# A planner's durations: other lengths for stores and loads, for products side by side, and for VectorE beside GpSimd

## The chip, the cores and the metric

The kernel runs on one core of one Trainium2 chip. The metric is the device time of one execution in microseconds (us). A core has TensorE (PE: matmuls and transposes; its weight loads are shown as PEld), VectorE (DVE), ScalarE (ACT), GpSimd (POOL) and SyncE (SP, which issues most DMAs). Each engine has a queue of instructions of its own, which it works off in order. Engines wait for one another by semaphores only.

## The reference, cut to what matters

Four layers run one after the other on x, 4 batches of 512 tokens by 512 channels in fp32, each conditioned on a vector of 512 per batch.

```
L0  h = LN(x)*(1+scale)+shift
    q = rope(h Wq^T) (16 heads of 32); c = h Wkd^T; k, v = c Wku^T, c Wvu^T (4 kv heads)
    x = x + softmax(window/global/causal-block mask of q k^T) v Wo^T
L1  RMS norm; 8 query heads of 64, one kv head, rope;  x += attention Wo^T
    RMS norm; x += (silu(h Wg^T) * (h Wu^T)) Wd^T          (width 2048)
L2  LN with scale and shift; q, k, v = h Wqkv^T + bias (16 heads of 32)
    q, k normalized to length 1 a head, q times exp(min(mul, log 100))
    x += gate1 * (softmax(q k^T + bias) v Wproj^T + b)
    x += gate2 * (gelu(h Wfc1^T + b) Wfc2^T + b)            (width 2048)
L3  8 groups of 64 channels, each: y = gelu(x W1 + b1) W2 + b2   (64 -> 256 -> 64)
    x = x + silu(LN(y)*(1+scale)+shift) out_W + out_b
```

The result is x, (4, 512, 512) in fp32.

## The kernel before, in words

All operands are fp32. A *product* is a 128x512 result built from four matmuls of 128x128 weights and 512 columns each; the trace shows each such matmul as two records. A softmax's probabilities are turned by 128x128 transposes on TensorE (`tr`, L360) into a PSUM bank, copied to SBUF as pT (`evict`, ACT or VectorE), and used as weights. Scores have 32 or 64 rows only, and four (or two) such products stand side by side in the array; so do the products of pT and v, which have 32 or 64 columns.

**Two streams.** The work of each batch is cut into stages: a01 (L0 and L1's attention), m1 (L1's MLP), a2 (L2's attention), m2 (L2's MLP and L3), for the last batches in halves. Stream A takes attention, stream M the MLPs of another batch, so that products of one fill TensorE while the softmax of the other runs. A stage is a Python generator that yields between steps; `interleave()` picks the next step. Weights come by 1 MB loads into two rings (tiles wa and wm). PSUM holds two pairs of banks for scores (tile two) and two single banks for each stream (tile bank). x has a ring of three buffers, in which stream M also keeps its kT and v.

**The planner.** Nothing is sent to an engine at once. `Clocks` (L161) writes down every operation with a planned start. `written` and `vacant` say from when an operand is there and from when a buffer is free, by the marks of earlier operations; `length` gives an operation's planned duration; `gap` looks for the first gap in the engine's list that is long enough; `plan` puts these together; `run` records an operation of ACT, VectorE, GpSimd or a DMA (all of these appear as L301 in the profile, loads as L367); `matmul` does the same for TensorE, with one running time `now` (matmuls appear as L354). `evict` plans a copy on ACT and on VectorE and takes the one that ends earlier. A stage's step is ready when its `Until` time is reached, so planned times also choose which step comes next. At the end all operations are sorted by planned start and emitted in that order (`tc.manual_schedule()`). The planned times are thus not waited for on the chip: they fix only the order of each engine's queue, the choice of ACT or VectorE, and, through the order, which buffer is reused when. What an engine really waits for are the data and buffers of the instruction at the head of its queue.

**Places that the prediction's steps touch.**

- a2's attention (`attention2`, with `attention` and `turn_full`): four scores products of 32 rows into two PSUM pairs (`two<-kT,nq`); on VectorE a custom instruction that adds the bias and takes the row's maximum (`probs<-two,late`, twice per half of the scores, and its accumulator's read neg); exponentials on ACT; the reciprocal inv; probs times inv on GpSimd; 16 transposes in four banks, each copied to pT. Products of stream M stand between.
- L2's normalization: q or k (tile t or mt), its squares, the sum ss on VectorE, a power on GpSimd (inv), t times inv on VectorE, transposes of t.
- `norm_steps`: statistics st and mv of x on VectorE, a power on GpSimd (rstd), then four tensor_scalar (nq or mn) with x from SBUF.
- L0's attention at the start (`attention0`): scores `two<-x,mn` (mn and x hold q and k there), maxima and exponentials into wm, wm times inv on GpSimd, transposes into hid. Products `bank<-wa_q,h` of batch 1's side go between, and they need the transposed nq (h).
- The load of a batch's x (`x<-in_x`) into a buffer of the ring, and the stores `out<-x`.

Of the kernel before, what the change touches and what calls it, by code (L numbers as in the profile page):

```python
# [58 lines left out]
class Ring:  # L59
# [3 lines left out]
    def __init__(self, load, made, pool, dram, tag, n, names):  # L63
        self.made, self.held = made, {}
        self.fetch, self.pool, self.dram, self.tag, self.n = load, pool, dram, tag, n
        self.names, self.tiles, self.taken, self.ahead = names, [], 0, n
# [94 lines left out]
class Clocks:  # L161
# [6 lines left out]

    def __init__(self):
        self.now, self.tiling, self.tables, self.queue = 0.0, None, None, 0.0  # L170
        self.busy = {"DVE": [], "ACT": [], "POOL": []}
        self.fixed, self.rings, self.program = {}, {}, []

# [38 lines left out]
    def gap(self, engine, ready, length):  # L212

        t = ready
        for a, b in self.busy[engine]:
            if b > t:
                if a - t >= length:
                    break
                t = b
        return t  # L220

    def length(self, engine, op, outs, ins, func):

        n = max(math.prod(v.shape[1:]) for v in outs[:1] + ins[:1])
        if engine == "DVE":
            held = 0.08 + (0.00073 if op == "tensor_scalar" and len(ins) > 1 else 0.00104) * n
        elif engine == "ACT":
            held = 0.03 + 0.00088 * n + (0.24 if len(outs) > 1 else 0.0)
            if func in self.SET and self.SET[func] != self.tables:
                held += self.LOAD_TABLE  # L230
        elif func == "pow":
            held = 0.3 + 0.157 * n
        else:
            held = 0.06 + (0.0023 if op == "tensor_tensor" else 0.0012) * n
        return held, held + 0.09

    def plan(self, engine, op, outs, ins, func=None):
        ready = max([self.written(*ins)] + [self.vacant(o) for o in outs])
        held, length = self.length(engine, op, outs, ins, func)
        return self.gap(engine, ready, held), held, length  # L240

    def run(self, engine, op, outs, ins, emit, func=None):
        if op == "dma_start":
            start = max([self.now, self.queue, self.written(*ins)] + [self.vacant(o) for o in outs])
            self.queue = start + max(math.prod(v.shape) for v in outs + ins) * 4 / 3.0e5
            end = self.queue + 2.0
        else:
            start, held, length = self.plan(engine, op, outs, ins, func)
            if func in self.SET:
                self.tables = self.SET[func]  # L250
            spans = [s for s in self.busy[engine] if s[1] > self.now - 60.0] + [(start, start + held)]
            self.busy[engine], end = sorted(spans), start + length
        for x in ins:
            self.mark(x, end + self.HOP, False)
        for x in outs:
            self.mark(x, end + self.HOP, True)
        self.program.append((start, len(self.program), emit))

    def matmul(self, out, left, right, begins, emit, turn=False):

        tiling = tuple(32 if n <= 32 else 64 if n <= 64 else 128 for n in (left.shape[0], math.prod(left.shape[1:])))
        if turn:
            tiling = (128, 128)
        start = max(self.now, self.written(left) + self.WEIGHTS, self.written(right))
        if out.tile.fresh and out.tile.before:
            start = max(start, out.tile.before.last)
        n = math.prod(right.shape[1:])
        self.now = start + (0.00085 if turn else 0.001676) * n * tiling[0] * tiling[1] / 16384
        if tiling != self.tiling:
            self.now += 0.2  # L270
        self.tiling = tiling
        self.mark(left, self.now, False)
        self.mark(right, self.now, False)
        self.mark(out, self.now + self.TAIL + self.HOP, True)
        self.program.append((start, len(self.program), emit))


# [31 lines left out]
def cond_seq_kernel(ctx: ExitStack, tc: tile.TileContext, a: dict, out: bass.AP):  # L309
# [66 lines left out]
    def evict(dst, src):  # L376

        ends = [(start + length) for start, _, length in (clocks.plan(e, "copy", [dst], [src]) for e in ("ACT", "DVE"))]
        if ends[0] <= ends[1]:
            scalar.copy(dst, src)  # L380
        else:
            vector.tensor_copy(dst, src)
# [1347 lines left out]
```

## Time and profile before

| what | value |
| --- | --- |
| three runs | 2469.41, 2475.03, 2479.4 us; median 2475.03 |
| the profiled execution, its own time | 2479.07 us |
| its span, from the first to the last instruction | 2477.3 us |
| mean granted TensorE clock | 0.991 |
| busy: ACT, GpSimd | 865.2 us (35%), 726.5 us (29%) |
| DMA | 154.17 MB, 62 GB/s on average |
| a 1 MB weight load, issue to landing | 5.1 to 5.7 us |

The profile shows each engine's busy time, the chain of instructions that ended last, and for each instruction how long its engine had been idle before it and what ended that. In rows of the timeline the columns are: start in us, duration in us (of all instructions that the row puts together), engine, line, operation, output<-input without buffer numbers, shapes, how many instructions, and in brackets the idle time before with its releaser. The durations of matmul records overlap: a record of 512 columns shows about 0.6 us, while the next one starts 0.43 us after it. A row with x8 is eight records. L301, L354, L360 and L367 are the lines of helpers that emit all recorded operations, so the tiles' names tell which step it is.

### The profile page before, as it was taken

Reading aid. Unit: us, or ns where it says so; the run is one execution under the profiler, and the core shown is the slowest. Engines: PE = TensorE matmul, PEld = TensorE weight load, DVE = VectorE, ACT = ScalarE, POOL = GpSimd, SP = SyncE. Lnnn points to the kernel's source line nnn. Section 1 sums busy time; section 2 is a strip of 40 time slices with the busy share of each in tenths; the row PEclk is TensorE's granted clock in tenths of the full one; section 3 lists DMA queues with packets and bytes.
Section 4 is the critical chain, followed back from the end, with each engine's and each line's share of the span. In section 5 each row is a group of like instructions: output and inputs, shape, how many; then the busy total and the mean of one; then the engine's idle time right before and its main releaser. Section 6 shows DMA issues by size and latency. Waiting matters only on the chain.

```text
span 2477.3 us, 33249 instructions
## 1 busy us (share of the span) xinstructions
PE 2413.0 (97%) x12564; PEld 1254.1 (51%) x12564; DVE 1123.4 (45%) x2902; ACT 865.2 (35%) x2076; POOL 726.5 (29%) x920
## 2 busy tenths in 40 slices
PE   7999999999999999999899999999999999999998
PEld 4555654444554555544355455554455544554444
DVE  5656552133653444534354444454455333653233
ACT  2745441003550442413354053332255203551312
POOL 5633320004322223323232221433232203532221
PEclk9999999999999999999899999999999999999999
DMA  3221212220113112120221212111211221112210
GB/s 110 69 73 52 85 35 85 85 72 35 39 48 106 52 52 70 40 74 27 76 68 39 86 52 75 49 56 56 85 35 52 83 92 51 35 54 84 72 56 22
DMA packets 83311, 154.17 MB, mean 62 GB/s; under 512 B 3584, under 2 KB 10784, under 8 KB 83152
## 3 DMA queue, kind: packets, MB, share of 16 engines
q1 hardware_dynamic: 82544, 151.83, 18.0%
q8 instruction: 100, 1.64, 0.3%
q14 instruction: 59, 0.48, 0.1%
q0 software_dynamic: 176, 0.15, 0.0%
q10 hardware_dynamic: 432, 0.07, 0.0%
HBM read 147.83 MB, written 4.21 MB: 61 GB/s over the span
## 4 chain that ended last, share of the span: by engine, by line
PE 91%; DVE 4%; ACT 2%; issue 1%; DMA 1%; POOL 1%; SPq 0%; POOLq 0%; DVEq 0%; ACTq 0%
PE bank L354 70%; PE bank L360 11%; PE two L354 10%; DVE probs L301 1%; ACT probs L301 1%; DVE pT L301 1%; PE two L360 0%; DVE nq L301 0%; ACT wm L301 0%; DVE mx L301 0%; DMA out<-x 0%; DMA wm<-in_units 0%; DMA x<-in_x 0%; POOL probs L301 0%; DVE mt L301 0%
## 5 line engine op out<-in xcount | busy, mean ns | idle before, releaser
L301 POOL TENSOR_SCALAR probs<-probs,inv 128x512 f32<-128x512 f32 (+4 forms) x544 | 316.4, 596 | 676.7 <-DVE inv L301 632.3
L301 ACT ACTIVATE probs<-probs,neg 128x512 f32<-128x512 f32 (+2 forms) x448 | 265.5, 594 | 221.0 <-DVE neg L301 212.4
L360 PEld LDWEIGHTS bank<-ident,probs 128*128 128x128 f32 (+2 forms) x1744 | 203.7, 141 | 175.0 <-issue 138.0
L360 PE MATMUL bank<-ident,probs 128*128 128x128 f32 (+2 forms) x1744 | 246.9, 276 | 8.0 <-DVE pT L301 7.0
L354 PE MATMUL bank<-mT,wm_gate 128*128 128x512 f32 x512 | 247.9, 596 | 0.0
L354 PE MATMUL bank<-mT,wm_up 128*128 128x512 f32 x512 | 247.6, 601 | 0.0
L354 PE MATMUL bank<-wm_down,hid 128*128 128x512 f32 x496 | 232.5, 597 | 0.0
L301 DVE CUSTOM_DVE_ANT_0 probs<-two,late 128x512 f32<-128x512 f32 x256 | 166.4, 688 | 80.1 <-PE two L354 47.1
L354 PE MATMUL bank<-wm_fc,hid 128*128 128x512 f32 x384 | 189.5, 593 | 0.0
L354 PE MATMUL bank<-mT,wm_fc 128*128 128x512 f32 x384 | 182.9, 595 | 0.0
L301 ACT COPY pT<-bank 128x512 f32<-128x512 f32 (+2 forms) x259 | 145.7, 577 | 78.2 <-PE bank L360 69.9
L354 PE MATMUL two<-kT,nq 32*128 32x512 f32 (+5 forms) x1088 | 150.5, 537 | 1.3 <-ACT probs L301 0.8
L301 ACT ACTIVATE mt<-bank 128x512 f32<-128x512 f32 x64 | 37.9, 591 | 318.5 <-PE bank L354 318.5
L301 DVE TENSOR_TENSOR x<-x,bank 128x512 f32<-128x512 f32 x98 | 66.8, 682 | 173.9 <-PE bank L354 173.9
L354 PEld LDWEIGHTS bank<-mT,wm_up 128*128 128x128 f32 x512 | 91.4, 191 | 100.1 <-issue 99.6
L354 PEld LDWEIGHTS bank<-pT,v 128*32 128x32 f32 (+2 forms) x3488 | 112.9, 116 | 49.4 <-issue 20.2
L354 PEld LDWEIGHTS bank<-mT,wm_gate 128*128 128x128 f32 x512 | 90.5, 190 | 91.5 <-issue 91.3
L354 PEld LDWEIGHTS bank<-wm_down,hid 128*128 128x128 f32 x496 | 89.0, 190 | 94.2 <-issue 93.0
L301 POOL TENSOR_TENSOR inv<-ss,neg_half 128x16 f32<-128x16 f32 x32 | 92.8, 2901 | 131.6 <-DVE ss L301 131.6
L354 PE MATMUL bank<-pT,v 128*32 128x128 f32 (+2 forms) x3488 | 130.8, 275 | 0.3 <-DVE coef_s L301 0.3
L354 PE MATMUL bank<-wa_q,h 128*128 128x512 f32 x272 | 129.9, 596 | 0.0
L301 POOL TENSOR_TENSOR rstd<-var,neg_half 128x4 f32<-128x4 f32 (+1 forms) x25 | 24.7, 992 | 356.8 <-DVE var L301 356.6
(278 smaller groups left out, 3390.5 us busy)
## 6 DMA issues: line engine op xcount, KB each, us to landing
wm_fc<-in_units SPq DMA_DIRECT2D x24, 1024.0 KB, 5.6
wm_gate<-in_units SPq DMA_DIRECT2D x16, 1024.0 KB, 5.5
wm_up<-in_units SPq DMA_DIRECT2D x16, 1024.0 KB, 5.3
wm_down<-in_units SPq DMA_DIRECT2D x16, 1024.0 KB, 5.6
wa_q<-in_units SPq DMA_DIRECT2D x10, 1024.0 KB, 5.1
wa_fc<-in_units SPq DMA_DIRECT2D x8, 1024.0 KB, 5.6
wa_o<-in_units SPq DMA_DIRECT2D x6, 1024.0 KB, 5.7
wa_k<-in_units SPq DMA_DIRECT2D x4, 1024.0 KB
```

What stands on the lines that cost most here:

```text
L301: return call(*map(real, args), **{k: real(x) for k, x in kw.items()})
L354: latest[0] = nc.tensor.matmul(real(out), lhsT=real(lhsT), rhs=real(rhs), **kw)
L360: latest[0] = nc.tensor.transpose(real(out), real(src), unit)
```

## The change

Only the planner's figures and rules change; every operation that a stage asks for is the same, and the planned times decide anew on order and on ACT or VectorE for the copies.

- `length`: a tensor_scalar on VectorE has the fast rate (0.00073 us an element) if none of its operands lies in PSUM, with one operand or more; before, if it had more than one input. One with an operand in PSUM has 0.00104 and 0.04 us for each input. GpSimd's operations other than tensor_tensor and power have 0.2 + 0.0009 us an element; before 0.06 + 0.0012.
- `plan`: such a fast tensor_scalar is held on VectorE until GpSimd's plan has a gap for it, and occupies VectorE meanwhile.
- `run`: a DMA has 340 GB/s in place of 300, and then 2.3 us (a load) or 8.0 us (a store) in place of 2.0.
- `matmul`: the 0.2 us at a change of tile size now also moves the start; products that stand side by side are marked as ended, and their operands as read, only when as many rounds of full length have passed as the run of such products has begun. TensorE's own running time is as before.

```diff
--- before.py
+++ after.py
@@ -168,6 +168,7 @@
 
     def __init__(self):
         self.now, self.tiling, self.tables, self.queue = 0.0, None, None, 0.0
+        self.begun, self.products, self.through = 0.0, 0, 0.0
         self.busy = {"DVE": [], "ACT": [], "POOL": []}
         self.fixed, self.rings, self.program = {}, {}, []
 
@@ -223,7 +224,11 @@
 
         n = max(math.prod(v.shape[1:]) for v in outs[:1] + ins[:1])
         if engine == "DVE":
-            held = 0.08 + (0.00073 if op == "tensor_scalar" and len(ins) > 1 else 0.00104) * n
+            held = 0.08 + 0.00104 * n
+            if op == "tensor_scalar" and self.fast(outs + ins):
+                held = 0.08 + 0.00073 * n
+            elif op == "tensor_scalar" and n > 16:
+                held += 0.04 * len(ins)
         elif engine == "ACT":
             held = 0.03 + 0.00088 * n + (0.24 if len(outs) > 1 else 0.0)
             if func in self.SET and self.SET[func] != self.tables:
@@ -231,19 +236,30 @@
         elif func == "pow":
             held = 0.3 + 0.157 * n
         else:
-            held = 0.06 + (0.0023 if op == "tensor_tensor" else 0.0012) * n
+            held = 0.06 + 0.0023 * n if op == "tensor_tensor" else 0.2 + 0.0009 * n
         return held, held + 0.09
+
+    def fast(self, views):
+
+        return all(not isinstance(v, View) or v.tile.tag not in ("bank", "two") for v in views)
 
     def plan(self, engine, op, outs, ins, func=None):
         ready = max([self.written(*ins)] + [self.vacant(o) for o in outs])
         held, length = self.length(engine, op, outs, ins, func)
-        return self.gap(engine, ready, held), held, length
+        start = self.gap(engine, ready, held)
+        if engine == "DVE" and op == "tensor_scalar" and self.fast(outs + ins):
+            wait = self.gap("POOL", start, held) - start
+            while self.gap("DVE", start, held + wait) > start:
+                start = self.gap("DVE", start, held + wait)
+                wait = self.gap("POOL", start, held) - start
+            return start, held + wait, length + wait
+        return start, held, length
 
     def run(self, engine, op, outs, ins, emit, func=None):
         if op == "dma_start":
             start = max([self.now, self.queue, self.written(*ins)] + [self.vacant(o) for o in outs])
-            self.queue = start + max(math.prod(v.shape) for v in outs + ins) * 4 / 3.0e5
-            end = self.queue + 2.0
+            self.queue = start + max(math.prod(v.shape) for v in outs + ins) * 4 / 3.4e5
+            end = self.queue + (8.0 if not outs else 2.3)
         else:
             start, held, length = self.plan(engine, op, outs, ins, func)
             if func in self.SET:
@@ -268,10 +284,18 @@
         self.now = start + (0.00085 if turn else 0.001676) * n * tiling[0] * tiling[1] / 16384
         if tiling != self.tiling:
             self.now += 0.2
-        self.tiling = tiling
-        self.mark(left, self.now, False)
-        self.mark(right, self.now, False)
-        self.mark(out, self.now + self.TAIL + self.HOP, True)
+            start += 0.2
+        side_by_side = 16384 // (tiling[0] * tiling[1])
+        if tiling != self.tiling or start > self.through + 0.01:
+            self.begun, self.products = start, 0
+        self.tiling, self.through = tiling, self.now
+
+        self.products += 1
+        rounds = (self.products - 1) // side_by_side + 1
+        end = self.now if side_by_side == 1 else max(self.now, self.begun + rounds * (self.now - start) * side_by_side)
+        self.mark(left, end, False)
+        self.mark(right, end, False)
+        self.mark(out, end + self.TAIL + self.HOP, True)
         self.program.append((start, len(self.program), emit))
 
 
```

## The prediction

> **What bounds the kernel now.** The page's first table and the chain come first. They answer one question: is any engine free to become faster?
>
> ```profile
> PE 2413.0 (97%) x12564; PEld 1254.1 (51%) x12564; DVE 1123.4 (45%) x2902; ACT 865.2 (35%) x2076; POOL 726.5 (29%) x920
> ...
> PE 91%; DVE 4%; ACT 2%; issue 1%; DMA 1%; POOL 1%; SPq 0%; POOLq 0%; DVEq 0%; ACTq 0%
> ```
>
> TensorE is busy for 2413.0 of 2477.3 us, and 91% of the chain is its own. The change leaves all products and transposes as they are, so it can reach only the rest: 2477.3 − 2413.0 = 64.3 us without a matmul, and what slow restarts hide inside the busy time. Then the waits of TensorE, which say who owns those 64 us (columns: engine, tile, line, what it waited for, total us, times, longest us):
>
> ```profile
> PE bank L360 <- DVE t L301: 16.1, 4, 12.1
> PE bank L354 <- DMA wm<-in_units: 9.3, 2, 9.2
> PE bank L360 <- DVE pT L301: 7.0, 21, 1.0
> PE bank L360 <- DVE nq L301: 4.8, 4, 2.9
> ```
>
> Of these, 9.2 us is the first weight's load, whose place doesn't change; 12.1 us is one stall, and 7.0 us is 21 small ones. A common VectorE instruction is not a bound: it matters only where TensorE waits for it.
>
> The built order of the changed kernel has the same 12564 matmul records (7674 instructions) on TensorE; changes of tile size go from 523 to 520. A change of tile size adds about 0.09 us between two records in before, so that is −0.3 us. SyncE's DMAs keep their order but for two adjacent swaps near the start; ACT gets 21 copies from PSUM that VectorE had (523 against 502), and 32 table loads against 30 (1.28 us each, on an engine 35% busy). So the time can only move through stalls, and I price these one after the other.
>
> **1. Scores marked later: the small stalls in a2 (−9.3 us).** The timeline of one of them:
>
> ```profile
> 2120.00 1.09 PE L360 MATMUL bank<-ident,probs 128*128 128x128 f32 x8
> ...
> 2120.83 0.68 DVE L301 CUSTOM_DVE_ANT_0 probs<-two,late 128x512 f32<-128x512 f32 x1
> 2120.93 1.02 PE L354 MATMUL bank<-wm_fc,hid 128*128 128x512 f32 x2
> ...
> 2121.44 0.69 DVE L301 COPY pT<-bank 128x512 f32<-128x512 f32 x1
> ...
> 2122.27 0.63 PE L360 MATMUL bank<-ident,probs 128*128 128x128 f32 x4 [0.32 <-DVE pT L301]
> ```
>
> After a group of scores come eight transposes, then one product (two records, 0.86 us), then four transposes that need the bank VectorE still has to copy. VectorE had taken two maxima (0.69 us each) of the new scores first. The idle time shown is 0.32 us; start to start, the step is 0.47 us longer than where nothing waits. In the trace this stands at 20 places (631.5 to 669.0 six, 2112 to 2212 twelve at 0.47; 1213.3 and 1804.5 at 0.37): 18 × 0.47 + 2 × 0.37 = 9.2 us, with 0.1 for a smaller one. In before's order every one of them has the pattern "eight transposes, one product, four transposes, one product, four transposes". In the changed order the 20 patterns read "eight, two products, four, one product, four": because the planner marks four side-by-side score products as ending later, it plans the VectorE copy later and puts another 0.86 us product before the waiting transposes. The copy ends at 2121.44 + 0.69 = 2122.13; with two products TensorE arrives at 2121.95 + 0.86 = 2122.81. The wait is covered by 0.5 us. The patterns with two products that before already has show no such wait. The product is moved, not added, so the next scores come no later in sum; their PSUM pair is free when the maxima are read, 2123.87 + 0.09, against a start at 2124.99. Bounds: −9.3 if all go, 0 if the wait only moves on; I take −9.3, since the two-product rows show none.
>
> **2. The stall of 12.1 us (0 us).** The plan of a store is now 8.0 us, so one expects the next load into its buffer to be planned later, and what hangs on it too.
>
> ```profile
> 1187.49 0.69 DVE L301 BATCH_NORM_STATS2 st<-x 128x6 f32<-128x512 f32 x1 [16.38 <-DMA x<-in_x]
> ...
> 1193.63 1.09 PE L360 MATMUL bank<-ident,t 128*128 128x128 f32 x4 [12.11 <-DVE t L301]
> ```
>
> VectorE stands 16.38 us before statistics of an x that is not there; the copy of kT, the sum ss, the power on GpSimd (2.90 us) and t stand behind them, and TensorE waits for t. x is late because its load (issue 1181.94, 5.53 us) waited for the stores out<-x (issued 1172.99 to 1175.5, 6.77 us on the chain). But in the changed order these statistics still stand ahead of the kT copy and of ss, and the load stands at the same place in SyncE's queue: `vacant` asks for the end of the tile that the planner's ring names as the one before in the buffer, and that is not the tile that the store reads. I therefore expect the stall again, 12.1 us, and the slow restart behind it: four records of 0.85 us for 0.43 us each (1196.22 3.54 us for x4), about 3 us in all up to 1199.6. Bounds: −15 (gone) to 0; I take 0, as the order is that of the row.
>
> The Trainium skill says (TensorE: Matmul & The Clock Gate, Part 1) that TensorE's clock halves after an idle window of about 3.4 us and returns after as long a busy one. This trace agrees after 12.11 us of idleness; for a gap between 1 and 9 us no row here shows it. By that rule a gap of 4.3 us, as in step 3, may add up to 1.7 us of lost rate; without it, nothing.
>
> **3. The start (+4 us).** A one-operand or SBUF-only tensor_scalar on VectorE is now planned to hold until GpSimd has a gap. The rows that bear on it are the four norms at 40.27 us, 5.16 us for x4, 1.29 us each beside GpSimd, where nq elsewhere takes 0.54 us. They feed the nq transposes of batch 1, for which TensorE waited 0.42 + 1.07 us at 44 and 45 us. In the changed order these 16 transposes stand behind the first scores of batch 0's attention, and so do the wa_q products: before has 8 of them (8 × 0.86 = 6.9 us) among the first four units of scores; the changed order has none until the fifth. In before the first unit takes from 54.52 (scores) to 59.3 (GpSimd's first four wm of the row 57.59 3.45 x8), 4.8 us. So in the changed order TensorE has 0.6 us of the next scores and then nothing until then: 4.8 − 0.6 = 4.2 us idle. ScalarE then gives a unit each 4 × 0.63 = 2.5 us, against 2.1 us of TensorE work a unit (7.6 us from the first scores to the first product, with the 16 transposes, over some 3.6 units): 0.4 us more a unit, 1.3 in three. From it I take off the nq waits, 1.5 us. Sum 4.2 + 1.3 − 1.5 = +4.0. The table load that now stands ahead of the first exponentials (1.28 us) lies beside other work if ScalarE reaches it early; bound 0 to +1.3, I take 0. Bounds of the step: −3 (a unit's wait is covered, and two of the 100 to 150 us stalls, 5.5 us together, go) to +9 (each unit waits its 2.5 us alone).
>
> **4. The rest (−0.7 us).** t now stands ahead of mt on VectorE at the two stalls of 2.0 us at 1139 and 1746: −0.2 each, as GpSimd's power ends only then; −0.3 from tile changes. The load waits at 2457 us and the end (3.9 us after the last matmul) have the same order: 0.
>
> **Sum.** −9.3 + 0 + 4.0 − 0.7 = −6.0 us. The profiled execution took 2479.07 us (span 2477.3, 1.8 around it), so it would become 2473.1. That execution is 4.0 us above the median of the runs, 2475.03; from the median the forecast is **2469.0 us**, its own range 2463 to 2476.
>
> **The rivals.**
> - *The waits move on* (2478). The copy is no longer waited for, but the later scores, planned after it, then meet a pair that the maxima still hold. For it: VectorE's 0.69 us maxima are the pacing step of a2 in every row above. Against: 1 us between the pair's release and the next scores. The 9.3 us are not won: 2475.0 + 4.0 − 0.7 = 2478.3.
> - *The long stall goes* (2454). If the store's length makes the statistics late in the real queue too, 12.1 + 3 us go: 2469.0 − 15.1 = 2453.9. Against it is the built order.
> - *Slower: the start runs without filler* (2489). Its mechanism is the chain scores, maxima, exponentials, power and wm, which takes 4.8 us a unit. If units don't overlap because each waits for its `two` pair or ScalarE, five units need 24 us for 7.6 us of TensorE work: +16.4, and the work at half rate +7.6. With −1.5 of nq, −9.3 and −0.7, and 1.3 of the table load: 2475.0 + 13.8 = 2488.8. It decides from the moment a unit's scores start only when the last unit's transposes are done. Against: before's units two and one overlap (scores at 54.52 and 56.96). The half rate here is that of the row at 1196.22. By the Trainium skill's rule (same page and section) it needs idle pieces of some 3.4 us each, which a chain of 4.8 us with 0.6 us of work in it would give; without it the rival is 2481.2.
> - *It does nothing* (2475). The order changes where nothing waits, and gains and losses at the start cancel those in a2.
>
> **Chances.** Forecast 0.48, moved waits 0.16, long stall gone 0.12, slower start 0.12, nothing 0.12. The range goes down to the long stall's 2453.9 and up to 2486, the start's bound of +9 without step 1's gain and with some spread of single runs (2469.4 to 2479.4). About 0.5%, 12.4 us, is what a measurement here can tell from no change: faster is the long stall and 0.04 of the forecast, 0.16; slower 0.12; the same 0.72.
>
> **What would show it.** Right: the line `bank L360 <- DVE pT` falls from 7.0 to below 2 us; `DVE t` keeps its 12.1; a gap of about 4 us ahead of the first wm transposes near 55 us; the nq line falls by 1.5. Wrong: pT keeps 7 us (step 1), t falls to 4 (step 2), no gap or several near 55 to 68 us (step 3).

## The result, and the profile after

The changed kernel takes **2463.13 us** (median of six runs, 2459.35 to 2466.56) against 2474.82 us before (six runs, 2469.41 to 2479.4). The ratio is 0.9951, 95% interval 0.9934 to 0.9968: 11.7 us less, where 6.0 us less was forecast. The profiled execution took 2465.19 us, with a span of 2463.4 us against 2477.3.

The first table of the page of the changed kernel, to be set beside that of before:

```profile
PE 2405.8 (98%) x12564; PEld 1257.0 (51%) x12564; DVE 1114.7 (45%) x2881; ACT 874.9 (36%) x2099; POOL 726.2 (29%) x920
```

TensorE has the same 12564 records, but is busy for 7.2 us less: a matmul that waits inside its run, or runs at a lower clock, is shown as busy (four transposes below take 1.52 us in one place and 0.60 in another). The rest of the 13.9 us of span is idle time. The waits of TensorE, changed kernel (the lines have moved: L360 is L384, L354 is L378, L301 is L325):

```profile
PE bank L384 <- DVE t L325: 15.6, 4, 11.9
PE bank L378 <- DMA wm<-in_units: 9.3, 2, 9.1
PE bank L378 <- DVE pT L325: 5.1, 3, 2.6
PE bank L384 <- DVE nq L325: 3.3, 2, 2.9
...
PE bank L384 <- POOL wm L325: 1.7, 1, 1.7
```

The transposes' wait for pT (7.0 us, 21 times, before) has gone from the list, the 12 us stall is still there, the nq line fell by 1.5 us, and a wait for the first wm is new (so are a few others of 1.4 to 1.9 us in the first 160 us, one of which raises the products' wait for pT from 3.3 to 5.1). Idle time alone doesn't add up to the change, so I used another measure. TensorE's trace is cut into runs of equal instructions (same tile and operand shapes, followed by the same kind); each run's time, from its first record to the first of the next run, is compared with the quickest tenth of such runs in all profiles of this study. What is above that, summed by stretch of the span, in us:

| kernel (profiled) | start, 0 to 400 us | a2's stretches | 1100 to 1200 us | from 2300 us | elsewhere |
| --- | --- | --- | --- | --- | --- |
| before | 44.2 | 15.1 | 17.7 | 18.1 | 13.0 |
| before, again (e10) | 48.2 | 15.7 | 16.1 | 16.4 | 12.9 |
| changed | 51.7 | 5.0 | 17.2 | 7.7 | 13.2 |
| e1 marks alone | 45.5 | 5.2 | 16.2 | 7.9 | 12.9 |
| e2 lengths and hold | 50.9 | 15.9 | 14.9 | 16.4 | 13.0 |
| e3 L3's order alone | 44.6 | 15.1 | 16.5 | 8.6 | 12.9 |
| e4 changed, no hold | 43.1 | 5.3 | 16.4 | 7.6 | 12.7 |
| e5 e4, right buffer of x | 39.9 | 5.5 | 2.5 | 7.5 | 12.4 |
| e7 L3 in two pairs | 46.4 | 15.0 | 16.1 | 8.4 | 13.0 |
| e8, e9 DMA times alone | 39.1, 44.8 | 15.0, 15.0 | 16.6, 16.4 | 16.4, 16.4 | 13.1, 13.0 |
| e11 marks, DMA times, buffer | 41.9 | 5.2 | 8.1 | 7.8 | 12.5 |

(a2's stretches are the hundreds that begin at 600, 1200, 1800 and 2000 to 2200 us.) Only differences between rows mean something, since the levels depend on how runs are matched. Changed against before: +7.5 at the start, −10.1 in a2, −10.4 at the end, −0.5 around the long stall. A reckoning without matched runs, the time by which TensorE has done the same amount of work, each record at its usual pace, gives +6.8, −10.0, −10.3 and −0.4. Three of these were in the forecast; the −10.4 was not. Two profiles of before differ by 4.0 at the start and by about 1.6 in two other columns, so the start's +7.5 is +3.5 to +7.5 (e3 and e7 have before's order up to 2400 us too, and lie between the two). The profiled execution of before was 4.3 us above its median, that of the changed kernel 2.1 above its own; so differences between profiles come out some 2 us larger than between medians.

**a2.** The changed kernel's timeline at the pattern that the prediction showed:

```profile
2124.32 1.09 PE L384 MATMUL bank<-ident,probs 128*128 128x128 f32 x8
...
2125.25 1.88 PE L378 MATMUL bank<-wm_fc,hid 128*128 128x512 f32 x4
...
2125.75 0.69 DVE L325 COPY pT<-bank 128x512 f32<-128x512 f32 x1
...
2126.97 0.60 PE L384 MATMUL bank<-ident,probs 128*128 128x128 f32 x4
```

Two products (x4) stand where one was. The copy ends at 2125.75 + 0.69 = 2126.44, and the four transposes start at 2126.97 with no wait in brackets: 0.53 us of cover.

**The end.** This is the first pair of 64-row products in L3's halves, before:

```profile
2408.14 1.13 PE L354 MATMUL two<-mT,wm_exp 64*128 64x256 f32 x6
...
2409.34 1.28 ACT L301 ACT_TABLE_LOAD   x1 [2.24 <-PE two L354]
2410.64 0.47 ACT L301 ACTIVATE hid<-two,vec 128x256 f32<-128x256 f32 x1
...
2411.17 2.85 PE L354 MATMUL two<-mT,wm_exp 64*128 64x256 f32 x10 [1.90 <-ACT hid L301]
```

and in the changed kernel:

```profile
2404.55 2.00 PE L378 MATMUL two<-mT,wm_exp 64*128 64x256 f32 x16
...
2405.78 1.28 ACT L325 ACT_TABLE_LOAD   x1 [2.25 <-PE two L378]
```

In before three of a group's four products (x6) ran, then the fourth waited until ScalarE had loaded a table and finished its first Gelu. In the changed kernel all eight products of two groups (x16) go through. The six such stretches, first record to the next kind of work, took 5.81, 2.38, 2.38, 3.18, 2.38 and 2.38 us before, 1.93, 1.06, 1.06, 1.93, 1.06 and 1.06 us after: 10.4 us. Before's list of waits showed about half of it:

```profile
PE two L354 <- ACT hid L301: 3.1, 3, 1.9
...
PE two L354 <- ACT pT L301: 1.8, 3, 0.6
```

**The start.** The changed kernel at the first scores of batch 0's attention:

```profile
49.20 0.50 PE L378 MATMUL two<-x,mn 32*128 32x128 f32 x8 [0.35 <-ACT x L325]
...
50.40 0.93 PE L378 MATMUL two<-x,mn 32*128 32x193 f32 x8 [0.69 <-DVE neg L325]
...
52.57 1.42 POOL L325 TENSOR_SCALAR wm<-wm,inv 128x128 f32<-128x128 f32 x4 [1.28 <-DVE inv L325]
...
53.00 1.52 PE L384 MATMUL bank<-ident,wm 128*128 128x128 f32 x4 [1.68 <-POOL wm L325]
```

and the same four transposes in before:

```profile
60.28 0.60 PE L360 MATMUL bank<-ident,wm 128*128 128x128 f32 x4
```

The products wa_q are missing between these rows, as forecast, but the gap shown is 1.68 us and not 4.2. The loss is spread: 0.69 us ahead of the second scores, 1.68 ahead of the transposes, and the transposes start 0.35 us apart, in 1.52 us for 0.60 in before, because GpSimd finishes the four wm 0.36 us apart (1.42 us for four) and the first transpose starts behind the first of them. From 49.20 us to the next scores at 54.45 TensorE does what takes it 1.7 us in before (0.53, 0.64 and 0.53 for the same records): some 3.5 us are lost. Meanwhile the clock falls. Busy time by windows of the same kernel (window, its length, busy time and records of PE, PEld, DVE, ACT and POOL, then the granted clock PEclk, the DMA share and GB/s):

```profile
49.00:53.00 4.00, 1.43 (x17) 0.94 (x17) 3.00 (x18) 3.97 (x17) 2.55 (x5) 0.94 0.00 0
53.00:57.00 4.00, 4.00 (x19) 2.60 (x20) 2.15 (x12) 3.23 (x14) 3.79 (x8) 0.50 0.02 6
57.00:61.00 4.00, 4.00 (x47) 3.22 (x46) 2.12 (x7) 2.46 (x7) 3.82 (x7) 0.71 0.01 2
```

After 4 us with TensorE busy for only 1.43, the clock is halved for almost 7 us (shares lost of 0.06, 0.50 and 0.29 in these windows of 4 us, at half rate). The same eight transposes inside it and behind it:

```profile
57.25 1.91 PE L384 MATMUL bank<-ident,nq 128*128 128x128 f32 x8
...
61.44 1.04 PE L384 MATMUL bank<-ident,nq 128*128 128x128 f32 x8
```

From 54.45 to 59.09 us eight scores, eight transposes of wm and eight of nq take 4.64 us; from 59.96 to 62.41 they take 2.45. So 2.2 us are lost here. How far this halved clock belongs to the order is open. Before's order has gaps of 0.42, 1.07, 0.46 and 0.46 us between 44 and 53 us; its clock is 0.61 from 45 to 49 us:

```profile
45.00:49.00 4.00, 3.52 (x17) 3.30 (x17) 1.98 (x4) 0.78 (x1) 0.81 (x2) 0.61 0.00 0
```

In e10 and e7, whose order is the same here and whose gaps agree within 0.01 us, the clock behind these gaps is another: from 45 to 57 us its mean is 0.86 in before, 0.61 in e10 and 1.00 in e7. In e2, the other kernel with the hold, it is 0.50 from 49 to 61 us; so both kernels that hold the norms have it for long, but one execution of each can't settle it.

### The profile page after: what moved, and what is told of

It reads as the page before. It is cut to its first block, busy times and chain, and to the rows that moved or that the text cites. A ratio compares the mean times of both kernels' runs of the same rounds, so it can differ in the third digit from the quotient of the medians.

```text
span 2463.4 us, 33258 instructions
## 1 busy us (share of the span) xinstructions
PE 2405.8 (98%) x12564; PEld 1257.0 (51%) x12564; DVE 1114.7 (45%) x2881; ACT 874.9 (36%) x2099; POOL 726.2 (29%) x920
## 4 chain that ended last, share of the span: by engine, by line
PE 94%; DVE 2%; ACT 1%; DMA 1%; POOL 1%; issue 1%; SPq 0%; POOLq 0%; ACTq 0%; DVEq 0%
PE bank L378 71%; PE bank L384 12%; PE two L378 10%; ACT probs L325 1%; PE two L384 0%; POOL inv L325 0%; ACT wm L325 0%; DVE mn L325 0%; DVE mx L325 0%; DMA out<-x 0%; DMA wm<-in_units 0%; DMA x<-in_x 0%; DVE nq L325 0%; DMA arow<-in_rows 0%; DVE t L325 0%
## 5 line engine op out<-in xcount | busy, mean ns | idle before, releaser
L325 POOL TENSOR_SCALAR probs<-probs,inv 128x512 f32<-128x512 f32 (+4 forms) x544 | 316.3, 596 | 690.9 <-DVE inv L325 647.5
L325 ACT ACTIVATE probs<-probs,neg 128x512 f32<-128x512 f32 (+2 forms) x448 | 265.5, 594 | 217.8 <-DVE neg L325 209.6
L384 PEld LDWEIGHTS bank<-ident,probs 128*128 128x128 f32 (+2 forms) x1744 | 205.9, 141 | 165.0 <-issue 138.5
L378 PE MATMUL bank<-mT,wm_up 128*128 128x512 f32 x512 | 246.9, 600 | 0.0
L384 PE MATMUL bank<-ident,probs 128*128 128x128 f32 (+2 forms) x1744 | 245.9, 275 | 0.9 <-POOL probs L325 0.5
L378 PE MATMUL bank<-mT,wm_gate 128*128 128x512 f32 x512 | 246.6, 595 | 0.0
L378 PE MATMUL bank<-wm_down,hid 128*128 128x512 f32 x496 | 231.7, 596 | 0.0
L325 DVE CUSTOM_DVE_ANT_0 probs<-two,late 128x512 f32<-128x512 f32 x256 | 166.4, 688 | 79.6 <-PE two L378 47.8
L378 PE MATMUL bank<-wm_fc,hid 128*128 128x512 f32 x384 | 187.7, 593 | 0.0
L378 PE MATMUL bank<-mT,wm_fc 128*128 128x512 f32 x384 | 182.2, 596 | 0.0
L325 ACT COPY pT<-bank 128x512 f32<-128x512 f32 (+1 forms) x264 | 147.9, 577 | 80.3 <-PE bank L384 72.3
L325 ACT ACTIVATE mt<-bank 128x512 f32<-128x512 f32 x64 | 37.9, 592 | 319.6 <-PE bank L378 319.6
L378 PE MATMUL two<-kT,nq 32*128 32x512 f32 (+5 forms) x1088 | 149.4, 539 | 0.8 <-ACT probs L325 0.8
L325 DVE TENSOR_TENSOR x<-x,bank 128x512 f32<-128x512 f32 x98 | 66.9, 682 | 169.5 <-PE bank L378 169.5
L378 PEld LDWEIGHTS bank<-mT,wm_up 128*128 128x128 f32 x512 | 91.4, 191 | 99.3 <-issue 98.9
L378 PEld LDWEIGHTS bank<-mT,wm_gate 128*128 128x128 f32 x512 | 91.0, 190 | 94.2 <-issue 94.0
L378 PEld LDWEIGHTS bank<-wm_down,hid 128*128 128x128 f32 x496 | 89.2, 190 | 95.9 <-issue 94.2
L378 PEld LDWEIGHTS bank<-pT,v 128*32 128x32 f32 (+2 forms) x3488 | 112.9, 116 | 49.1 <-issue 30.3
L325 POOL TENSOR_TENSOR inv<-ss,neg_half 128x16 f32<-128x16 f32 x32 | 92.8, 2901 | 128.0 <-DVE ss L325 128.0
L378 PE MATMUL bank<-pT,v 128*32 128x128 f32 (+2 forms) x3488 | 130.5, 274 | 0.0
L378 PE MATMUL bank<-wa_q,h 128*128 128x512 f32 x272 | 128.1, 596 | 1.2 <-DVE neg L325 1.2
L325 DVE COPY pT<-bank 128x512 f32<-128x512 f32 (+1 forms) x175 | 117.8, 683 | 22.2 <-PE bank L384 21.5
```

The costliest lines, as they stand in the source:

```text
L325: return call(*map(real, args), **{k: real(x) for k, x in kw.items()})
L378: latest[0] = nc.tensor.matmul(real(out), lhsT=real(lhsT), rhs=real(rhs), **kw)
L384: latest[0] = nc.tensor.transpose(real(out), real(src), unit)
```

## The experiments

**e1: the marks alone.** Before, with the changed `matmul` (its fields in `__init__` too) and nothing else.

```diff
...
-        self.mark(out, self.now + self.TAIL + self.HOP, True)
...
+        self.products += 1
+        rounds = (self.products - 1) // side_by_side + 1
+        end = self.now if side_by_side == 1 else max(self.now, self.begun + rounds * (self.now - start) * side_by_side)
...
+        self.mark(out, end + self.TAIL + self.HOP, True)
```

> The kernel before with the planner's matmul part alone (later marks for side-by-side products, start moved at a tile change). Theory: this part carries all of the gain, -10.0 us from the pT stalls of a2 and -10.4 us from the 64-row products of L3's halves, and none of the loss at the start: 2474.8 - 20.4 = 2454.4 us, excess of TensorE's steps in the first 400 us as in before (43.2 us), the line 'bank <- DVE pT' under 2 us. Rival (the gain needs the other parts too, or the start's loss comes with the marks): 2463 us, as the whole change.

Measured 2459.29 us against 2475.93; ratio 0.9928 (0.9915 to 0.9942), 16.6 us less. That is 4.9 us more than the theory's 2454.4, whose terms came from profiles. In the table a2 and the end fall as in the whole change, and the start stays as before. The rival, that the other parts are needed, falls: this part alone is at least as fast as the whole change (its median is 3.8 us lower, while the times of both overlap a little, 2455.14 to 2461.2 against 2459.35 to 2466.56).

**e2: lengths and hold alone.** The changed kernel with before's `matmul` and before's DMA times.

```diff
-            self.queue = start + max(math.prod(v.shape) for v in outs + ins) * 4 / 3.4e5
-            end = self.queue + (8.0 if not outs else 2.3)
+            self.queue = start + max(math.prod(v.shape) for v in outs + ins) * 4 / 3.0e5
+            end = self.queue + 2.0
...
```

> The kernel before with the new lengths of VectorE and GpSimd and the hold of VectorE for GpSimd, but with before's matmul marks and DMA times. Theory: only the start changes, +7.5 us: 2482 us, pT line at 7 us, L3 halves slow as before. Rival (the lengths take part in the gain): under 2475 us.

Measured 2484.13 against 2475.93 us; ratio 1.003 (1.0018 to 1.0042), 8.2 us more. The start's column rises, a2 and the end keep their waits (pT 6.1 us, 20 times). These parts alone make the kernel slower, by 0.3%.

**e3: L3's order alone.** Before, with the four products of a group in L3's halves marked as ended together in the plan.

```diff
+            for f in range(2) if n < S else ():
+                for j in range(2):
+                    clocks.mark(bank(j, f), clocks.now + clocks.TAIL + clocks.HOP, True)
             for f in range(2):
                 for j in range(2):
                     bias = V_B1 + 4 * p + 2 * j + f
```

> The kernel before with one thing: in L3's halves the four 64-row products of a pair are marked as ended together, so that the first Gelu is queued, and counted, after the fourth product. Theory (the fourth product waits for the Gelu only because it comes after it in the program): -10.4 us, 2464.4 us, the six groups cost 1.93 and 1.06 us instead of 3.2 to 5.8 and 2.38. Rival (the wait is for the pair of banks or for the table load, whatever the order): within 2 us of 2474.8.

Measured 2467.35 against 2475.93 us; ratio 0.9967 (0.9954 to 0.9979), 8.6 us less, where the theory had 10.4. Of the columns only the last changes by more than two profiles of before differ (18.1 to 8.6). So the wait came with the order of the Gelu and the fourth product.

**e7: why the order makes a wait.** The Gelu reads the first 256 columns of one bank, the fourth product writes the last 256 of the other bank of the pair. Before, with the products for f = 0 and f = 1 in two pairs; in the built order the Gelu still stands ahead of the fourth product in the first three groups (the trace doesn't show this order, which runs over two engines):

```diff
...
-            banks = [two_banks() for _ in range(2 if n == S else 1)]
+            banks = [two_banks() for _ in range(2)]
...
-                return banks[f][:, j, :] if n == S else banks[0][:, j, f * n : (f + 1) * n]
+                return banks[f][:, j, 0:n]
```

> The kernel before, where in L3's halves the products with f = 0 and those with f = 1 go to two PSUM pairs instead of two halves of one pair's banks; the first Gelu still comes ahead of the fourth product in ACT's and the program's order in the first three groups. Theory (the fourth product waits because the Gelu reads the same pair, though other columns): the waits of 'two <- ACT hid' inside a group go, about 2463 to 2468 us, less what the next group waits for both pairs. Rival (the wait is by queue order whichever pair): 2475 us, the groups at 2.38 us.

Measured 2465.68 against 2475.81 us; ratio 0.9956 (0.9942 to 0.997), 10.1 us less. The first group, in the timeline of e7:

```profile
2408.67 1.13 PE L354 MATMUL two<-mT,wm_exp 64*128 64x256 f32 x8
```

Eight records without a break, where before had six and a wait. With the order kept, the wait is thus by the PSUM tile that both instructions use, not by queue order as such, nor by columns. In L3's second half one stretch still takes 3.00 us, for 3.18 in before: there the second group waits 0.51 us until ScalarE's Gelus of the first have freed a pair. The planner's marks are by columns, so it planned the Gelu beside the product and could not see the wait.

**e4: the changed kernel without the hold.**

```diff
         start = self.gap(engine, ready, held)
-        if engine == "DVE" and op == "tensor_scalar" and self.fast(outs + ins):
-            wait = self.gap("POOL", start, held) - start
-            while self.gap("DVE", start, held + wait) > start:
-                start = self.gap("DVE", start, held + wait)
-                wait = self.gap("POOL", start, held) - start
-            return start, held + wait, length + wait
         return start, held, length
```

> The changed kernel without the hold of VectorE's tensor_scalar until GpSimd has a gap (the new lengths, DMA times and marks stay). Theory (the hold delays the four norms at the start and takes the wa_q products from between the first scores): the loss at the start goes, 2463.1 - 7.5 = 2455.6 us, and no gap before the first wm transposes. Rival (the start is lost through the new lengths themselves): 2463 us.

Measured 2451.52 against 2475.93 us; ratio 0.9899 (0.9884 to 0.9914): 11.6 us better than the changed kernel, where the theory had 7.5. In the table 8.6 of it lie at the start, and some of that is the clock, which differs between executions. The norms on VectorE, in the changed kernel and then in e4:

```profile
43.53 0.94 DVE L325 TENSOR_SCALAR nq<-x,mv,rstd 128x512 f32<-128x512 f32 x1 [3.97 <-POOL rstd L325]
...
45.66 0.53 DVE L325 TENSOR_SCALAR nq<-x,mv,rstd 128x512 f32<-128x512 f32 x1
...
50.59 0.98 DVE L325 TENSOR_SCALAR nq<-x,mv,rstd 128x512 f32<-128x512 f32 x1
...
54.85 0.53 DVE L325 TENSOR_SCALAR nq<-x,mv,rstd 128x512 f32<-128x512 f32 x1
```

```profile
43.16 0.94 DVE L319 TENSOR_SCALAR nq<-x,mv,rstd 128x512 f32<-128x512 f32 x1 [4.49 <-POOL rstd L319]
...
45.29 2.69 DVE L319 TENSOR_SCALAR nq<-x,mv,rstd 128x512 f32<-128x512 f32 x3
```

The hold saves 3.63 − 2.98 = 0.65 us of VectorE, which has time to spare, and hands over the last norm 7.4 us later (55.38 against 47.98). With it go the products that need it. In e4 they are back between the scores, and TensorE's clock stays at 1.00 from 45 to 65 us:

```profile
51.73 0.60 PE L372 MATMUL two<-x,mn 32*128 32x193 f32 x6
52.26 3.70 PE L372 MATMUL bank<-wa_q,h 128*128 128x512 f32 x8
55.80 0.60 PE L378 MATMUL bank<-ident,wm 128*128 128x128 f32 x4
```

**e5 and e6: the long stall.** The planner is told which buffer the last x goes into; e5 is e4 with this edit, e6 is before with it (stores planned at 2.0 us).

```diff
         xs[b] = buf("x", 3)
+        if b == 3:
+            xs[b].tile.before = xs[0].tile
```

> The changed kernel without the hold, and the planner is told that the last batch's x goes into the buffer of batch 0's x, so that the 8.0 us of the stores delay its planned load and the statistics of it on VectorE. Theory (the 12 us stall is an order of VectorE's queue: statistics of an x that has not landed, ahead of the copy of kT and the sum ss): the stall and the slow restart go, -13 to -15 us against the kernel without the hold: 2451.5 - 14 = 2437 us; line 'bank <- DVE t' falls from 15.8 to about 4 us. Rival (another wait takes its place, since the x still lands at the same time): 2451 us.

> The kernel before with that same word on the buffer of the last batch's x, and nothing else: the stores keep their planned 2.0 us. Theory (it needs the longer store as well): only one copy of kT moves ahead of the statistics, the sum ss still stands behind them, so the stall keeps about 12 us: 2475 us. Rival (the right buffer alone is enough): 2461 us.

e5: 2438.62 against 2475.81 us; ratio 0.9847 (0.9831 to 0.9864), 12.9 us better than e4. e6: 2474.66 against 2475.81; ratio 0.9992 (0.9982 to 1.0002), no change. The end of the load's wait in e5:

```profile
1172.22 0.60 PE L378 MATMUL bank<-ident,t 128*128 128x128 f32 x4
...
1178.37 0.69 DVE L319 BATCH_NORM_STATS2 st<-x 128x6 f32<-128x512 f32 x1 [7.15 <-DMA x<-in_x]
```

VectorE still waits 7.15 us for x, but the transposes of t ran 6 us ahead of the statistics, which nobody needs soon; the line `bank <- DVE t` is 3.7 us, the longest 1.7. With the true buffer and stores planned at 8.0 us the order moves (e5); with the true buffer and 2.0 us (e6) the sum ss stays behind the statistics and the wait is 11.2 us. e6 lacks the new marks and lengths as well, so that the store's length makes this difference by itself is argued, not shown.

**e8, e9 and e10: DMA times alone, twice, and before again.** e8 and e9 are before with the changed `run` (the reverse of e2's diff); e10 is before.

> The kernel before with the new times of loads and stores alone (340 GB/s, 2.3 and 8.0 us). Theory: nothing that TensorE waits for changes its place: 2475 us within 3, the 12 us stall included. Rival (the store's 8.0 us moves the stall): 2461 us.

> The kernel with the new DMA times alone, once more, for a second profile of the same order. Theory (TensorE reached its full clock at 18 us and not at 25 to 29 us by chance of that execution): the first 16 records wa_q,mT take between 8 and 9.5 us, as in the other kernels, and the last nq transposes' place stands some 3 us later. Rival (the order does it): 7.1 us again.

> The kernel before, for a second profile. Both theories: wa_q,mT 8 to 9.5 us; it says how far two profiles of one order differ (half a us to 2 us at the start, nothing in a2 and in L3's halves).

e8: 2471.74 against 2475.81 us, ratio 0.9984 (0.9974 to 0.9994); the long stall stays. That is 4.1 us less where none was expected, and just outside the theory's 3 us. Its profile gained it at the start, where TensorE came to full clock early: the first 16 records wa_q,mT took 7.11 us, against 8.38 in before. e9, the same order, has 7.78 us (neither the theory's 8 to 9.5 nor the rival's 7.1), 44.8 in the start's column and one time of 2474.9; e10 has 9.26 us and 2478.78, and its start differs from before's by 4.0 us where 2 at most was expected. The order brings these records forward by at least a us (20.24 and 21.56 against 22.65 and 22.70); the rest of the difference between e8 and e9 varied from one execution to the next. How much of the 4.1 us a longer series would keep is open.

**e11: marks, DMA times and the buffer, without the new lengths.**

> The kernel before with the new marks, the new DMA times and the word on the buffer of the last x, without any of the new lengths of VectorE and GpSimd. Theory (each is worth the same beside the others: -16.6 or -20 of the marks, -13 of the buffer, 0 to -4 of the DMA times): 2438 to 2445 us. Rival (the new lengths without the hold are worth something of their own): over 2445 us, and e5 stays ahead.

Measured 2444.5 against 2476.29 us; ratio 0.987 (0.9854 to 0.9886). It is in the theory's band, at its upper end; the rival is right in part, since e5 stays 5.9 us ahead. Around the long stall the table has 8.1 us here and 2.5 in e5, because here VectorE's mt still stands behind the statistics:

```profile
1180.65 0.69 DVE L310 BATCH_NORM_STATS2 st<-x 128x6 f32<-128x512 f32 x1 [9.18 <-DMA x<-in_x]
...
1181.26 0.67 DVE L310 SCALAR_TENSOR_TENSOR mt<-mt,bank 128x512 f32<-128x512 f32 x1
...
1181.98 1.12 PE L363 MATMUL bank<-mT,wm_gate 128*128 128x512 f32 x2 [3.53 <-DVE mt L310]
```

With the new lengths mt stands ahead of them (in e5 it starts at 1170.54, the statistics at 1178.37): that saves the 3.5 us of wait and the slower records behind it (two records of mT,wm_gate take 1.91 us from 1184.19, and 1.02 in e5).

## Why the prediction was right in sign and short in size

1. **a2 (−9.3 forecast).** Right in mechanism and size: −10.1 by the table, the pT line gone, cover 0.53 us for a forecast 0.5 (the two times that the prediction sets against each other, 2122.13 and 2122.81, are 0.68 apart, since 2121.95 is a record's end; start to start, 2120.93 + 2 × 0.86 = 2122.65, it is 0.52). e1 shows that the marks do it, e2 and e8 that the other parts don't. The rival "the waits move on" falls.
2. **The long stall (0 forecast).** Right: 11.9 us are left of 12.1. The change has the longer store but not the true buffer, and e5 against e4 shows that the buffer's name is needed; e6 shows that the name alone is not enough. The rival of 2454 us was a possible kernel, but another one.
3. **The start (+4.0 forecast).** The sign and the cause were right (the norms held, the fillers late; e4 and e2), and +7.5 (+3.5 by the second profile of before) lies within the step's bounds. The chain was as long as forecast: from the scores at 49.20 to the end of GpSimd's first four wm at 53.99 it took 4.8 us. But the transposes don't wait for all four wm, so only 1.68 us of it shows as a gap, and TensorE lost some 3.5 us there for a forecast 4.2. A further gap of 1.24 us among the next units, ahead of 64.15, is about the forecast 1.3 (0.4 us a unit makes 1.2 in three), and the nq waits fell by 1.5 as forecast. Behind the first gap came what the step put outside the sum, the halved clock: 2.2 us in this execution. The sentence that no row shows this for a gap between 1 and 9 us was wrong too: in before the clock is 0.61 from 45 to 49 us, right after the nq waits of 0.42 and 1.07 us. The Trainium skill's Part 1 (TensorE: Matmul & The Clock Gate) would want an idle window of some 3.4 us; here 1.43 us of work in 4.00, with no single gap above 1.7, came before the halved clock, so the trace doesn't agree. The Trainium skill's section on a second HAM failure mode (TensorE: Matmul & The Clock Gate; HAM is its name for what sets this clock), where frequent short idle times between groups of matmuls make the clock swing, fits these rows better; why the same gaps were followed by the full clock in e7 stays open.
4. **The rest (−0.7 forecast).** This is the step that failed: of what lies behind 2300 us it named only the load waits at 2457 us and the tail behind the last matmul, at 0, and L3's halves have no term. The marks also moved the first Gelu of a group behind the fourth product in L3's halves, worth −8.6 (e3, timed) to −10.4 us (profile). The lines `two <- ACT hid` and `two <- ACT pT` stood in before's list of waits, below the four that the prediction quoted, and weren't followed.

So the forecast of 2469.0 missed the measured 2463.1 by a left-out gain of about 9 to 10, against which the start lost up to 3.5 more than forecast. That 2463.1 still lies at the lower edge of the forecast's own range, 2463 to 2476, is in part luck: two misses went against each other.

## What to carry to other kernels

Where a planner's durations only fix queue order, cost each change at the few places where an engine really waits, and go through all of TensorE's waits, the short lines too; compare start to start, since the idle time in brackets showed half of the L3 stalls and two thirds of those in a2. A correction that makes the plan truer to one engine (VectorE held for GpSimd) can cost more elsewhere: it saved 0.65 us on an engine with slack and delayed TensorE's filler. Profile one order more than once before you explain a few us at the start: two profiles of before differ there by 4.0 us. And a plan must know the buffers and dependences that the real program has: a longer store counts only on the right buffer, and marks by columns miss a wait that is by tile.

## What the runs showed of the hardware that was not expected

- TensorE's granted clock fell to 0.50 behind a stretch in which it was busy for 1.43 of 4.00 us, with gaps of 0.35, 0.69 and 1.68 us, and stayed there for almost 7 us.
- The same order with the same gaps of 0.42 to 1.07 us between 44 and 53 us had a mean clock of 0.86, 0.61 and 1.00 from 45 to 57 us in three executions (before, e10, e7).
- With one order, the first 16 records of wa_q,mT took 8.38, 9.26 and 9.55 us in three executions (before, e10, e7): after 3 to 6 of them the distance from one record to the next falls from 0.85 to 0.43 us, so when this happens varies from one execution to the next.
